# Layer 0 of a four-layer graph network: sums of exponentials by thirds of a half, and the last 20 keys held three times in row groups

## The chip, the cores and the metric

The kernel runs on one core of a Trainium2 chip. The time is that of one execution on the device in microseconds (us); the median of three runs is given. One execution more was taken with the hardware profiler, and every line of a profile shown here is of such an execution. The engines are PE (TensorE, with its weight loads, PEld), DVE (VectorE), ACT (ScalarE), POOL (GpSimd) and SP (SyncE, which here issues most DMAs).

## What is computed

Four layers work on 2708 nodes with 512 features each, with one adjacency matrix `adj` (2708 x 2708, about 1.2% ones and a full diagonal). After each layer, x is added and the rows are normalized. The change is in layer 0 alone, an encoder and a decoder over the same attention. Cut to what matters, with N = 2708, H = 4 heads, D = 128:

```python
Xw  = einsum('hnd,hde->hne', Xh, W)
f1  = einsum('hnd,hd->hn', Xw, V[:, 0, :, 0])
f2  = einsum('hnd,hd->hn', Xw, V[:, 1, :, 0])
sig = sigmoid(f1[:, :, None] + f2[:, None, :])
att = softmax(where(adj != 0, adj * sig, -inf))      # over the keys; both patterns are adj
Xa  = einsum('hij,hjd->hid', att, Xw)                # attention pass a
emb = mlp_block(batchnorm(Xa))                       # elu, a product with 512 x 512, batch norm
Y   = einsum('hij,hjd->hid', att, emb)               # attention pass c, the same att
out = mlp_block(elu(Y @ W.T))
x   = layernorm(x + out)
```

Layers 1 (mean over neighbours), 2 and 3 (attention over all nodes) follow; nothing in them is touched.

## The kernel before, in words

**Tiles.** Keys (the index j that is summed over) lie on the partitions, in 22 tiles: 21 of 128 keys and a last one of 20, since 2708 = 21 x 128 + 20. Queries (i) lie along the free axis, in two halves of 1354. The four heads are taken in two pairs. So `attention_pass` (from line 270) has four rounds, (half 0, pair 0), (half 0, pair 1), (half 1, pair 0), (half 1, pair 1), and each goes over the 22 key tiles `jt`. It runs twice: as pass a with the values `xw`, and as pass c with `emb`.

**One key tile.** `form` loads a 128 x 1354 piece of the adjacency (L300, on SP's queue; four buffers in pass a). With pair 0 in pass a it first turns zeros into a very negative number on DVE (L303, L304) and stores the piece to DRAM for later rounds (L307, on POOL's queue). Then ACT makes tanh of f1 + f2 for both heads (L313, two instructions), DVE combines it with the adjacency (L321), and ACT takes the exponential (L322). The result `t`, 128 keys x 2 heads x 1354 queries, has four buffers. PE then makes the weighted sums (L366): for each head three products of 452 or 450 columns, with a 128 x 128 piece of the values as weights, accumulated over the 22 tiles in PSUM. The accumulators are three tiles po0, po1, po2, one for each third of the half, each with one bank for each head of the pair.

**Sums of exponentials.** In pass a alone, PE also adds up the exponentials over the keys (L389): for each head four products of 340 columns, with a 128 x 32 block of ones as weights. Each quarter of the half goes to its own 32 PSUM rows (0, 32, 64, 96), and so to its own 32 columns of the array. With pair 0 this is done for every tile. With pair 1 it is done for each of the first six tiles, and then once for two tiles, which DVE adds up first in place (L383). The last tile is the second of such a two.

**The end of a round.** In pass a, `keep` copies the accumulators to `ft` (L466: the first and last thirds on DVE, the middle ones on ACT), takes the sums at least at a tiny number (L473), sends them through DRAM to be inverted and spread over the partitions (L476 to L483, then `spread_sums`, L260 and L264), and leaves eight small steps (L490 and L491: scale a quarter of a head, take its statistics) for the next round's tiles. In (half 0, pair 1) it also makes a small product, ps_beta (L434), in the slot of po0. In the last round there is no next one: maxima (L505), reciprocals (L506), a product that spreads a row over the partitions (L512, in two of the accumulator slots in turn) and the eight steps (L520, L521) are done on the spot. In pass c, `decode` scales the accumulators on DVE (L660), adds the shift and masks (L672), and goes on to ps_y (L676), the elu (L403 to L408), and after pair 1 the decoder's product (L687).

**Kept tiles.** In pass a the exponentials of some key tiles are stored to DRAM (L358): tiles 5, 13 and 21 of pair 0, and 3, 9, 15 and 21 of pair 1. Pass c reloads these (L360) and makes the others anew. The last tile, 21, is so kept in all four rounds.

**What sets the order.** The program is written once in the order of the work; a tile framework's scheduler puts each engine's instructions in a fixed order when the kernel is built, from dependencies, priorities and the buffers of each pool. [...] A PSUM accumulator is taken again when all that read it are done.

The dimensions behind the lines that are changed:

```python
NHALF, HB, HP = 2, 3, 2            # halves, thirds of a half, heads of a pair
HW = 2 * ((N + 3) // 4)            # 1354
BW = 2 * ((HW + 2 * HB - 1) // (2 * HB))   # 452
SQ = 4
SW = 2 * ((HW + 2 * SQ - 1) // (2 * SQ))   # 340
```

Layers 2 and 3 already hold the values of the last 20 keys in four copies, at partitions 0, 32, 64 and 96, and make their products there in four row groups (L1090, records marked `20*128`).

Of the kernel before, what the change touches and what calls it, by code (L numbers as in the profile page):

```python
# [8 lines left out]
F32 = mybir.dt.float32  # L9
# [4 lines left out]
ALU = mybir.AluOpType  # L14
# [3 lines left out]
P = 128  # L18
# [3 lines left out]
TINY = 1e-30  # L22
# [7 lines left out]
def gnn_stack_kernel(  # L30
# [25 lines left out]
    nc = tc.nc  # L56
    N, F = x.shape
    H = w0.shape[1]
    C = F // P
    NT = (N + P - 1) // P  # L60
    NFULL = N // P
    BLOCKS = [(i * P, min(P, N - i * P)) for i in range(NT)]
    BANK = 512

    const = ctx.enter_context(tc.tile_pool(name="const", bufs=1))
    big = ctx.enter_context(tc.tile_pool(name="big", bufs=1))
# [59 lines left out]
    CHUNKS = [(h0 + q0, w) for (h0, _), ch in zip(HSPAN, HCH) for q0, w in ch]  # L126
    NCH = len(CHUNKS)

    SQ = 4
    SW = 2 * ((HW + 2 * SQ - 1) // (2 * SQ))  # L130
    SCH = [[(q * SW, min(SW, w - q * SW)) for q in range(SQ)] for _, w in HSPAN]

# [18 lines left out]
    with ExitStack() as l0:  # L151
# [7 lines left out]
        }  # L159
        f1_d = dram.tile([H, N], F32, name="f1_d")  # L160

        SR = SQ * SW // 17
        assert SR <= P and SR * 17 == SQ * SW
        sum_d = dram.tile([H, NHALF, SQ, SW], F32, name="sum_d")
        rs_d = dram.tile([H, NHALF, SQ, SW], F32, name="rs_d")

# [3 lines left out]
        ones32 = p0.tile([P, 32], F32, name="ones32")  # L170
        nc.vector.memset(ones32, 1.0)
        f2h = p0.tile([P, NT, H], F32, name="f2h")

        bm1 = p0.tile([P, C], F32, name="bm1")
        nc.vector.tensor_scalar(bm1, prm_sb[:, MB_DEC, :], 1.0, None, ALU.subtract)
# [10 lines left out]
        def project(att, psum):  # L186

            held = p0.tile([P, C, F], F32, tag="mlp_w", name="held").rearrange("p c f -> p (c f)")  # L190
            w0x = held[:, : H * (P + 2)].rearrange("p (h e) -> p h e", h=H)
            nc.sync.dma_start(w0x[:, :, :P], w0)
            v12 = att.tile([P, H, 2], F32, tag="v12", name="v12", bufs=1)
            nc.sync.dma_start(v12[:, :, 0], v1)
            nc.sync.dma_start(v12[:, :, 1], v2.rearrange("(h e) -> e h", h=H))
            for c in range(C):
                nc.sync.dma_start(xT_sb[:, c, :], xT[c * P : (c + 1) * P, :])
            pv = psum.tile([P, H, 2], F32, tag="psm0", name="pv")
            for h in range(H):
                nc.tensor.matmul(  # L200
                    pv[:, h, :], w0T_sb[:, h, :], v12[:, h, :], start=True, stop=True
                )
            nc.vector.tensor_copy(w0x[:, :, P:], pv)
            wv1 = held[:, H * (P + 2) : H * (2 * P + 2)].rearrange("p (h e) -> p h e", h=H)
            nc.vector.tensor_copy(wv1, w0x[:, :, P : P + 1].to_broadcast([P, H, P]))
            f1b = att.tile([P, HP, HW], F32, tag="f1b", name="f1b")
            for k in range(HP):
                for q, (q0, w) in enumerate(HCH[0]):
                    pf = psum.tile([P, HP, BANK], F32, tag=f"po{q}", name="pf")[:, k, :]
                    nc.tensor.matmul(  # L210
                        pf[:, :w], wv1[:, k, :], xT_sb[:, k, q0 : q0 + w], start=True, stop=True
                    )
                    copy = nc.scalar.copy if q % 2 else nc.vector.tensor_copy
                    copy(f1b[:, k, q0 : q0 + w], pf[:, :w])
            for ci, (c0, w) in enumerate(CHUNKS):
                pf = psum.tile([P, BANK], F32, tag=f"psm{ci % 2}", name="pf")
                for h in range(H):
                    nc.tensor.matmul(
                        pf[32 * h : 32 * h + 32, :w],
                        wv1[:, h, :32],  # L220
                        xT_sb[:, h, c0 : c0 + w],
                        start=True,
                        stop=True,
                    )
                f1c = att.tile([P, BW], F32, tag="rs", name="f1c")
                nc.vector.tensor_copy(f1c[:, :w], pf[:, :w])
                nc.gpsimd.dma_start(f1_d[:, c0 : c0 + w], f1c[0 : 32 * H : 32, :w])
            for jt, (j0, n) in enumerate(BLOCKS):
                pxw = psum.tile([P, H // HP, BANK], F32, tag=f"po{jt % HB}", name="pxw")
                pv = pxw[:, :, : HP * (P + 2)].rearrange("p a (k e) -> p a k e", k=HP)  # L230
                for h in range(H):
                    nc.tensor.matmul(
                        pv[:n, h // HP, h % HP, :],
                        xT_sb[:, h, j0 : j0 + n],
                        w0x[:, h, :],
                        start=True,
                        stop=True,
                    )
                copy = nc.vector.tensor_copy if jt % 3 == 2 else nc.scalar.copy
                copy(  # L240
                    xw[:n, jt, :].rearrange("p (a k d) -> p a k d", a=H // HP, k=HP),
                    pv[:n, :, :, :P],
                )
                nc.vector.tensor_scalar(
                    f2h[:n, jt, :].rearrange("p (a k) -> p a k", k=HP),
                    pv[:n, :, :, P + 1],
                    0.5,
                    None,
                    ALU.mult,
                )  # L250
            return f1b

        def spread_sums(att, hf, p):
# [16 lines left out]
        def attention_pass(values, first, att, psum, finish, f1b=None):  # L270
# [23 lines left out]
            def form(hf, p, jt, att, prepare, f1b, tv):  # L294
# [3 lines left out]
                a = att.tile([P, HW], F32, tag="a", name="a", bufs=4 if first else 3)  # L298
                src = adjT if prepare else adj_d
                nc.sync.dma_start(a[:n, :w], src[j0 : j0 + n, h0 : h0 + w])  # L300
                if prepare:
                    z = att.tile([P, HW], F32, tag="z", name="z", bufs=1)
                    nc.vector.tensor_scalar(z[:n, :w], a[:n, :w], 0.0, None, ALU.is_equal)  # L303
                    nc.vector.scalar_tensor_tensor(  # L304
                        a[:n, :w], z[:n, :w], -BIG, a[:n, :w], ALU.mult, ALU.add
                    )
                    nc.gpsimd.dma_start(adj_d[j0 : j0 + n, h0 : h0 + w], a[:n, :w])  # L307
                if not first and p == (jt in KEPT[0]):
                    count(hf, jt, att, a)

# [14 lines left out]
            for hf, (h0, w) in enumerate(HSPAN):  # L325
                for p in range(H // HP):
# [20 lines left out]
                    for jt, (j0, n) in enumerate(BLOCKS):  # L347
# [5 lines left out]
                        tv = t[:n, :, :w]  # L353
                        kept = kept_d.get((hf, p, jt))
                        if kept is None or first:
                            form(hf, p, jt, att, prepare, f1b, tv)
                            if kept is not None:
                                nc.gpsimd.dma_start(kept[:n, :, :w], tv)  # L358
                        else:
                            nc.sync.dma_start(tv, kept[:n, :, :w])  # L360
                            if p == 0 and jt in KEPT[1]:
                                count(hf, jt, att)
                        for k in range(HP):
                            h = HP * p + k
                            for q, (q0, qw) in enumerate(HCH[hf]):
                                nc.tensor.matmul(  # L366
                                    po[HB * k + q][:, :qw],
                                    values[:n, jt, h * P : (h + 1) * P],
                                    t[:n, k, q0 : q0 + qw],
                                    start=(jt == 0),  # L370
                                    stop=(jt == NT - 1),
                                )
# [73 lines left out]
        with (  # L446
# [7 lines left out]
            def keep(hf, p, po, sums):  # L454
# [15 lines left out]
                if not final:  # L470
                    for k in range(HP):
                        h = HP * p + k
                        nc.vector.tensor_scalar(  # L473
                            sm[k][:, :SW], sums[k][:, :SW], TINY, None, ALU.max
                        )
                        nc.gpsimd.dma_start(sum_d[h, hf], sm[k][0 : 32 * SQ : 32, :SW])  # L476
                    part = slice(HP * p, HP * (p + 1)), hf
                    few = att.tile([SR, HP, 17], F32, tag="few", name="few", bufs=1)
                    wide = "h r w -> h (r w)"
                    cut = "h (s e) -> s h e"  # L480
                    nc.sync.dma_start(few, sum_d[part].rearrange(wide).rearrange(cut, s=SR))
# [20 lines left out]
                    )  # L502
                for k in range(HP):
                    h = HP * p + k
                    nc.vector.tensor_scalar(sm[k][:, :SW], sums[k][:, :SW], TINY, None, ALU.max)  # L505
                    nc.vector.reciprocal(sm[k][:, :SW], sm[k][:, :SW])  # L506
                    nc.gpsimd.dma_start(rs_d[h, hf], sm[k][0 : 32 * SQ : 32, :SW])
                    for r, (q0, qw) in enumerate(SCH[hf]):
                        pb = psum.tile(
                            [P, HP, BANK], F32, tag=f"po{1 + (SQ * k + r) // 2 % 2}", name="pb"  # L510
                        )[:, r % 2, :]
                        nc.tensor.matmul(  # L512
                            pb[:, :SW],
                            sel[:, r * P : (r + 1) * P],
                            sm[k][:, :SW],
                            start=True,
                            stop=True,
                        )
# [37 lines left out]
        with (  # L556
# [36 lines left out]
            for ci, (c0, w) in enumerate(CHUNKS):  # L593
# [34 lines left out]
                while turned < NT and sum(BLOCKS[turned]) <= c0 + w:  # L628
# [3 lines left out]
                        nc.tensor.transpose(tp[:n, c, :], ft[:, c, j0 : j0 + n], ident)  # L632
                    nc.scalar.copy(emb[:n, turned, :], tp[:n].rearrange("p c d -> p (c d)"))
                    turned += 1


            scale2, mean2 = batch_scale(stats, MG_ENC, "bn2")
# [231 lines left out]
    GW = max(w for _, w in GSPAN)  # L869
    GB = max(len(g) for g in GROUPS)  # L870

    Q = 32
    REST = N - NFULL * P
    assert 0 < REST <= Q and C * Q == P
    quarters = const.tile([P, C, Q], F32, name="quarters")
    for c in range(C):
        nc.vector.tensor_tensor(
# [535 lines left out]
```

## Time and profile before

| what (before) | value |
|---|---|
| median of three runs | 3387.1 us (3385.58 to 3390.83) |
| the profiled execution's own time | 3383.28 us |
| its span, from the first to the last instruction | 3381.5 us |
| mean granted clock of PE, as a share of full | 0.984 |
| PE busy (matmul records) | 3304.0 us |
| DVE, ACT, POOL busy | 1988.8, 1339.6, 127.6 us |
| pass a, from its first weighted sum to its last sum of exponentials | 53.7 to 586.6 us |
| pass c, from its first weighted sum to its last | 703.6 to about 1181 us |
| layer 1's first product | 1244.0 us |

A group's row gives line, engine, operation, what is written and read (`20*128` is 20 active rows and 128 active columns of the array), sizes and count, then the busy time and the mean of one in ns, then the engine's idle time just before and what ended most of it. An fp32 product is two records. Matmuls are pipelined, and their ends are modelled; for the pace of PE, starts are to be compared, not lengths.

### The profile page before, as it was taken

What the parts mean: (1) busy time and instruction counts of PE and PEld (TensorE: products, weight loads), DVE (VectorE), ACT (ScalarE), POOL (GpSimd) and SP (SyncE); (2) the same over time, 40 slices, a digit from 0 to 9 for tenths busy, and PEclk for the clock granted to TensorE, in tenths of its full rate; (3) what the DMA queues carried; (4) which work ended last, traced back from release to release, by engine and by line L of the source; (5) the groups of instructions that cost most, each with busy time, mean ns of one, the idle gap of its engine ahead of it and who ended that gap; (6) DMA issues with size and microseconds to landing.
All of it is one profiled execution on the core that took longest, in us unless ns stands there. A gap on an engine that the chain in (4) does not pass through costs nothing.

```text
span 3381.5 us, 30504 instructions
## 1 busy us (share of the span) xinstructions
PE 3304.0 (98%) x10981; PEld 1761.1 (52%) x10981; DVE 1988.8 (59%) x3227; ACT 1339.6 (40%) x1491; POOL 127.6 (4%) x205
## 2 busy tenths in 40 slices
PE   8999999999999989999999999999999999999998
PEld 4444444544444445886555555444455555555554
DVE  7867977767687585445136666777253442543533
ACT  6877887568858743001133333333011010110110
POOL 1100100000000000000010000000000000000001
PEclk9998999999999999999999999999999999999999
DMA  7655753335524331550034444554111111111100
GB/s 279 246 164 166 276 184 114 120 103 168 184 82 160 126 106 61 140 136 19 0 114 125 116 127 128 145 148 112 58 50 35 44 33 44 37 33 44 35 23 19
DMA packets 167483, 364.03 MB, mean 108 GB/s; under 512 B 20374, under 2 KB 111194, under 8 KB 164100
## 3 DMA queue, kind: packets, MB, share of 16 engines
q1 hardware_dynamic: 152596, 298.43, 29.3%
q0 software_dynamic: 14736, 63.66, 5.0%
q8 instruction: 86, 1.41, 0.2%
q14 instruction: 65, 0.53, 0.0%
HBM read 298.34 MB, written 63.35 MB: 107 GB/s over the span
## 4 chain that ended last, share of the span: by engine, by line
PE 74%; issue 15%; DVE 6%; DMA 2%; ACT 2%; POOL 1%; SPq 0%; POOLq 0%; DVEq 0%; ACTq 0%
PE po L1090 22%; PE ps_s L996 17%; PE po L366 8%; PE ps_nb L842 7%; PE ps_wide L908 4%; PE ps_hid L113 2%; PE ps_sup L1233 2%; DVE t L321 2%; PE ps_o L1168 2%; PE ps_dec L687 2%; PE ps_mlp L601 1%; DMA a<-adj_d 1%; POOL adj_d L307 1%; PE ps_s L991 1%; ACT t L313 1%
## 5 line engine op out<-in xcount | busy, mean ns | idle before, releaser
L321 DVE SCALAR_TENSOR_TENSOR t<-t,a 128x2708 f32<-128x2708 f32 (+1 forms) x162 | 479.3, 2975 | 144.8 <-ACT t L313 143.3
L313 ACT ACTIVATE t<-f1b,f2h 128x1354 f32<-128x1354 f32 (+1 forms) x324 | 445.3, 1414 | 91.2 <-PE psm L389 47.1
L366 PE MATMUL po<-t,xw 128*128 128x452 f32 (+3 forms) x1056 | 433.0, 561 | 3.9 <-ACT t L322 3.9
L366 PE MATMUL po<-t,emb 128*128 128x452 f32 (+3 forms) x1056 | 416.3, 552 | 10.7 <-ACT t L322 9.2
L322 ACT ACTIVATE t<-t 128x2708 f32<-128x2708 f32 (+1 forms) x162 | 396.7, 2452 | 52.0 <-DVE t L321 50.5
L1090 PE MATMUL po<-sup,e 128*128 128x512 f32 x882 | 410.0, 601 | 5.2 <-DVE e L1277 5.2
L1090 PE MATMUL po<-e,xs 128*128 128x384 f32 (+1 forms) x1176 | 407.5, 489 | 0.0
L996 PE MATMUL ps_s<-q,hT 128*128 128x384 f32 (+1 forms) x1176 | 403.5, 489 | 0.0
L1331 DVE SCALAR_TENSOR_TENSOR e<-a_cols,ps_s 128x384 f32<-128x384 f32 (+1 forms) x154 | 85.6, 556 | 419.7 <-PE ps_s L996 396.6
L366 PEld LDWEIGHTS po<-t,emb 128*128 128x128 f32 (+1 forms) x1056 | 201.6, 193 | 220.1 <-issue 199.2
L366 PEld LDWEIGHTS po<-t,xw 128*128 128x128 f32 (+1 forms) x1056 | 197.8, 193 | 224.9 <-issue 211.4
L996 PEld LDWEIGHTS ps_s<-q,hT 128*128 128x128 f32 x1176 | 222.6, 190 | 161.5 <-issue 6.2
L1090 PEld LDWEIGHTS po<-e,xs 128*128 128x128 f32 x1176 | 221.6, 190 | 157.2 <-issue 6.0
L1090 PEld LDWEIGHTS po<-sup,e 128*128 128x128 f32 x882 | 162.0, 192 | 176.8 <-issue 148.3
L996 PE MATMUL ps_s<-hT 128*128 128x384 f32 (+1 forms) x672 | 229.2, 488 | 1.0 <-ACT sup L1240 0.7
L93 ACT ACTIVATE ln_rstd<-ln_rstd 128x1 f32<-128x1 f32 x88 | 17.2, 201 | 497.4 <-DVE ln_rstd L92 496.9
L1273 ACT ACTIVATE a_cols<-a_cols,neg_big 128x384 f32<-128x384 f32 (+1 forms) x154 | 94.8, 616 | 249.7 <-DMA a_cols<-in_adjT_dram 208.4
L842 PE MATMUL ps_nb<-hid_hi,at 128*128 128x512 f32 x484 | 188.1, 390 | 0.4 <-DVE at L836 0.4
L842 PE MATMUL ps_nb<-hid_lo,at 128*128 128x512 f32 x484 | 187.8, 389 | 0.0
L1067 ACT COPY nmax<-pb 128x384 f32<-128x384 f32 (+1 forms) x14 | 6.7, 479 | 430.5 <-PE pb L1054 349.8
L996 PEld LDWEIGHTS ps_s<-hT 128*128 128x128 f32 x672 | 125.8, 190 | 97.1 <-issue 18.0
L1085 DVE TENSOR_TENSOR acc<-acc,e 128x384 f32<-128x384 f32 (+2 forms) x294 | 162.9, 554 | 12.3 <-ACT e L1075 2.3
(223 smaller groups left out, 3474.1 us busy)
## 6 DMA issues: line engine op xcount, KB each, us to landing
a<-adj_d SPq DMA_DIRECT2D x116, 677.0 KB
a_cols<-in_adjT_dram SPq DMA_DIRECT2D x378, 192.0 KB
a<-in_adjT_dram SPq DMA_DIRECT2D x42, 677.0 KB
adj_d<-a POOLq DMA_DIRECT2D x42, 677.0 KB, 4.5
raw<-in_adjT_dram SPq DMA_DIRECT2D x105, 256.0 KB
kept<-t POOLq DMA_DIRECT2D x10, 1354.0 KB, 6.6
t<-kept SPq DMA_DIRECT2D x10, 1354.0 KB
a_cols<-in_adjT_dram SPq DMA_DIRECT2D x63, 202.0 KB
```

The costliest lines, as they stand in the source:

```text
L113: nc.tensor.matmul(ps[:n], xt[:, c, :n], w[:, c, :], start=(c == 0), stop=(c == C - 1))
L313: nc.scalar.activation(tv[:, k, :], f1b[:n, k, :w], AF.Tanh, bias=f2h[:n, jt, h : h + 1], scale=0.5,)
L321: nc.vector.scalar_tensor_tensor(tv, tv, GUARD, ab, ALU.add, ALU.mult)
L322: nc.scalar.activation(tv, tv, AF.Exp, scale=0.5)
L366: nc.tensor.matmul(po[HB * k + q][:, :qw], values[:n, jt, h * P : (h + 1) * P], t[:n, k, q0 : q0 + qw], start=(jt == 0), stop=(jt == NT - 1),)
L842: nc.tensor.matmul(pos[it], at, half[:, jt, :], start=(jt == 0 and k == 0), stop=(jt == NT - 1 and k == 1),)
L908: nc.tensor.matmul(ps[:, :width], w(c, o), xt(c), start=(c == 0), stop=(c == C - 1),)
L996: nc.tensor.matmul(ps[:, :w], keys[:, c, j0 : j0 + P], st["q"][:, c, :], start=(c == 0), stop=(c == C - 1),)
L1085: nc.vector.tensor_tensor(acc, acc, e[:m], ALU.add)
L1090: nc.tensor.matmul(out, lhsT, rhs, start=(k == 0), stop=(k == NT - 1))
L1273: nc.scalar.activation(a, a, AF.Identity, bias=neg_big[: a.shape[0]], scale=1.0e30)
L1331: nc.vector.scalar_tensor_tensor(e, a, 2.0, ps, ALU.mult, ALU.add)
```

## The change

Two things are changed in layer 0.

The sums of exponentials are made by thirds of a half (`SQ = HB = 3`, so `SW = 452`) where they were made by quarters. For each head there are three products of 452 columns on PSUM rows 0, 32 and 64. All that follows from it has thirds too: maxima and reciprocals on 96 rows of 452, the small steps that are left for the next round (six of 452 or 450 columns for eight of 340 or 334), the statistics, and the way through DRAM (113 rows of 12 numbers for each head in place of 80 rows of 17). In the last round the spreading product has a slot of its own for each of its six results.

The last 20 keys lie in three copies, at partitions 0, 32 and 64 (84 rows with the gaps, `HR`). `form` loads the adjacency's last 20 rows three times and 12 rows of other keys into each of the two gaps, five DMAs for one; tanh, combination and exponential run on 84 rows. The values get their copies by DMAs on POOL's queue (`copies`: `xw` and `f2h` after the projection, `emb` after the encoder). Pass c reloads the last tile three times. In the weighted sums of the last tile, third q of the queries is made on row group q, so that the three products of a head use three row groups of the array; the columns and the accumulators are the same as before. The sums of exponentials still take the first 20 rows alone.

```diff
+    Q = 32
+    REST = N - NFULL * P
...
-    SQ = 4
+    SQ = HB
...
-        SR = SQ * SW // 17
-        assert SR <= P and SR * 17 == SQ * SW
+        SR = next(k for k in range(P, 0, -1) if SQ * SW % k == 0)
+        SE = SQ * SW // SR
+        SP = 32 * SQ
...
+        nc.vector.memset(f2h[:, NT - 1, :], 0.0)
+        HR = (HB - 1) * Q + REST
+        def copies(rows):
+            for r in range(1, HB):
+                nc.gpsimd.dma_start(rows[r * Q : r * Q + REST], rows[:REST])
...
+            copies(xw[:, NT - 1, :])
+            copies(f2h[:, NT - 1, :])
...
                 nc.sync.dma_start(a[:n, :w], src[j0 : j0 + n, h0 : h0 + w])
+                if n < P:
+                    for r in range(HB):
+                        if r > 0:
+                            nc.sync.dma_start(
+                                a[r * Q : r * Q + n, :w], src[j0 : j0 + n, h0 : h0 + w]
+                            )
+                        if r + 1 < HB:
+                            nc.sync.dma_start(
+                                a[r * Q + n : (r + 1) * Q, :w], src[: Q - n, h0 : h0 + w]
+                            )
+                    n = HR
...
-                            form(hf, p, jt, att, prepare, f1b, tv)
+                            rows = n if n == P else HR
+                            form(hf, p, jt, att, prepare, f1b, t[:rows, :, :w])
...
-                            nc.sync.dma_start(tv, kept[:n, :, :w])
+                            for r in range(0, P if n == P else HB * Q, P if n == P else Q):
+                                nc.sync.dma_start(t[r : r + n, :, :w], kept[:n, :, :w])
...
                             for q, (q0, qw) in enumerate(HCH[hf]):
+                                r = 0 if n == P else q * Q
                                 nc.tensor.matmul(
                                     po[HB * k + q][:, :qw],
-                                    values[:n, jt, h * P : (h + 1) * P],
-                                    t[:n, k, q0 : q0 + qw],
+                                    values[r : r + n, jt, h * P : (h + 1) * P],
+                                    t[r : r + n, k, q0 : q0 + qw],
...
-                    nc.vector.reciprocal(sm[k][:, :SW], sm[k][:, :SW])
-                    nc.gpsimd.dma_start(rs_d[h, hf], sm[k][0 : 32 * SQ : 32, :SW])
+                    nc.vector.reciprocal(sm[k][:SP, :SW], sm[k][:SP, :SW])
+                    nc.gpsimd.dma_start(rs_d[h, hf], sm[k][0:SP:32, :SW])
                     for r, (q0, qw) in enumerate(SCH[hf]):
-                        pb = psum.tile(
-                            [P, HP, BANK], F32, tag=f"po{1 + (SQ * k + r) // 2 % 2}", name="pb"
-                        )[:, r % 2, :]
+                        slot = SQ * k + r
+                        pb = psum.tile([P, HP, BANK], F32, tag=f"po{slot // 2}", name="pb")
+                        pb = pb[:, slot % 2, :]
...
+            copies(emb[:, NT - 1, :])
```

## The prediction

> **What bounds the kernel now.** I read the page first: which engine is full, and where the clock falls.
>
> ```profile
> PE 3304.0 (98%) x10981; PEld 1761.1 (52%) x10981; DVE 1988.8 (59%) x3227; ACT 1339.6 (40%) x1491; POOL 127.6 (4%) x205
> ...
> PEclk9998999999999999999999999999999999999999
> ...
> L366 PE MATMUL po<-t,xw 128*128 128x452 f32 (+3 forms) x1056 | 433.0, 561 | 3.9 <-ACT t L322 3.9
> L366 PE MATMUL po<-t,emb 128*128 128x452 f32 (+3 forms) x1056 | 416.3, 552 | 10.7 <-ACT t L322 9.2 <-DVE ot L660 1.4
> ```
>
> TensorE (PE) is full, and the weighted sums of both attention passes (L366) waited only 3.9 and 10.7 us in all. Layer 0 takes the first 1,240 us; the change touches only its passes, a (53.7 to 586.6 us) and c (703.6 to 1181 us). In pass a a PE microsecond counts in full, unless a wait takes its place. Next, the timeline of PE where one pair of heads ends and the next begins (start, length, engine, line, what, records):
>
> ```profile
> 171.32 4.82 PE L366 MATMUL po<-t,xw 128*128 128x452 f32 x12
> 176.07 1.35 PE L389 MATMUL psm<-t,ones 128*32 128x340 f32 x16
> 177.35 5.89 PE L366 MATMUL po<-t,xw 20*128 20x452 f32 x12
> 183.17 2.49 PE L389 MATMUL psm<-t,ones 20*32 20x340 f32 x16
> 185.59 7.58 PE L366 MATMUL po<-t,xw 128*128 128x452 f32 x12
> ```
>
> From start to start, a full tile of keys costs 4.75 us of weighted sums (12 records, two for each fp32 product, 0.377 us apart) and 1.28 us of sums of exponentials. The last 20 keys cost as many records on 20 of 128 rows, and from there all slows. The table by stretch (PE busy, ..., granted clock, DMA) tells why:
>
> ```profile
> 171.32:177.35 6.03, 6.03 (x32) 2.62 (x29) 4.94 (x2) 5.20 (x4) 0.00 (x0) 1.00 0.36 116
> 177.35:181.00 3.65, 3.65 (x14) 1.90 (x11) 0.32 (x1) 3.65 (x3) 0.00 (x0) 0.99 0.60 193
> 181.00:185.59 4.59, 4.59 (x21) 1.04 (x19) 2.52 (x5) 2.18 (x4) 0.19 (x1) 0.50 0.01 1
> 185.59:191.00 5.41, 5.41 (x11) 2.52 (x8) 5.27 (x3) 4.58 (x3) 0.97 (x2) 0.50 0.20 23
> ```
>
> After 3.65 us of 20-row products, with PE busy throughout, the clock is halved, and stays so into the next tile. The same follows the other 20-row tiles (half clock in 310.6 to 327.7 and in 812.4 to 815.8, for two). I call these places ends, and the start of the last 20 keys T.
>
> [...] layer 3's last keys (8 records of 384 columns) start at 2564.27 and the next product at 2565.13, 0.86 us against 2.58 for full rows. Three column groups no run shows yet. [...]
>
> **Sums in thirds: a loss on the path.** Before, eight 340-column products fill four column groups: four rounds for 16 records, 1.28 us. After, six 452-column products fill three: again four rounds, now wider. The nearest row is f1 (L218), 16 records of 450 or 452 columns in four groups:
>
> ```profile
> 32.61 1.72 PE L218 MATMUL pf<-xT_sb,held 128*32 128x452 f32 x16
> 34.26 2.84 PE L232 MATMUL pxw<-held,xT_sb 128*128 128x130 f32 x23
> ```
>
> Start to start 1.65 us, so 0.37 more a group. Below, 0.30, if only part of the width shows; [...] I take 0.37. The 1152 records of L389 are 72 groups: 26.6 us. The built order also splits two of the first four groups (1 product, 12 projections, 5 products): 0.85 each for an extra round, 1.7. In the second pair of heads of each half PE waited for exponentials 3.9 us in all; ACT's pair of tiles (2 x (2 x 1.41 + 2.45) = 10.5 us) then has more room: 2.9 us absorbed. Sum: **+25.4**.
>
> **The last 20 keys in row groups: PE time.** Twelve records in three groups are four rounds of 0.377 plus 0.22 of start (0.86 - 2 x 0.32 in the layer-3 row): 1.73 us in place of 4.75, at all eight ends. But what comes next was hidden under those 3 us.
>
> **End of pass a's first pairs (T = 177.35, 451.02).** PE after: T+1.73, sums to T+3.4, first product of the new pair to T+4.15; the second needs accumulator po1, copied out by ACT (L466). ACT's order, unchanged by the build: tanh of a tile whose buffer comes free at T, then both copies.
>
> ```profile
> 177.24 2.46 ACT L322 ACTIVATE t<-t 128x2708 f32<-128x2708 f32 x1 [0.69 <-DVE t L321]
> 179.61 2.72 ACT L313 ACTIVATE t<-f1b,f2h 128x1354 f32<-128x1354 f32 x2
> 182.24 0.95 ACT L466 COPY ft<-po 128x452 f32<-128x452 f32 x2
> ```
>
> That is T+4.9 to T+5.85, and it doesn't move, for what feeds it is released at T. So PE stands 1.75 us, and its five other products end at T+9.7. In T to T+5.9 PE then has 1.73 us on 60 rows, 1.65 on 20, 0.75 in full and a stall: [...] I expect the clock to halve again, for a shorter time (5 us at half = 2.2 to 2.5 lost[...]). With 2.2, T+11.9; before, 193.09 = T+15.74. Gain 3.8, and the last group's 0.37 is hidden by the wait: **-4.2 each**.
>
> **End of the first half (T = 306.60).** The sums need the last two tiles added (L383), which can't start before T, as it overwrites what PE reads until then:
>
> ```profile
> 306.78 2.97 DVE L383 TENSOR_TENSOR t<-t 20x2708 f32<-20x2708 f32 x1
> 309.67 1.55 DVE L304 SCALAR_TENSOR_TENSOR a<-z,a 128x1354 f32<-128x1354 f32 x1
> 311.15 0.61 DVE L466 COPY ft<-po 128x452 f32<-128x452 f32 x1
> ```
>
> Before, PE reached its sums at T+5.4, with all that past. After, it is ready at T+1.73 and starts them at about T+3.75 (the build puts a 0.86 step ahead of the add); then one product, then ps_beta (L434, 32 records, 3.6 us at full clock, as at 612.5) which needs the copies, T+7.1; with the five other products T+14.6, sums T+15.9 at 1.28. [...] the clock halves here as well (estimate 3.5 lost): T+19.2 against 330.45 = T+23.85: **-4.7**.
>
> **End of pass a (T = 579.21).** The chain from the add through L466, the maxima, two reciprocals (2.2 us at 340 columns, 3.0 at 452) to the last statistics is DVE's. It starts when the add does, at T+0.2; 1.5 more of reciprocals, 0.7 less for six scalings and statistics (452 columns, 1.24 a pair) in place of eight (1.01). The accumulator slots no longer repeat, which saves the 0.8 that DVE waited for PE. **0**.
>
> **Pass c.** First end: DVE copies out (L660) at T+2.07 when its tile work is done, po0 is free at T+3.4; gain of 2 us less stalls and the same half clock: **-0.7**. Second and third: PE already waits for these copies.
>
> ```profile
> 1069.63 2.98 DVE L321 SCALAR_TENSOR_TENSOR t<-t,a 128x2708 f32<-128x2708 f32 x1 [4.35 <-ACT t L313]
> 1072.75 3.83 DVE L660 SCALAR_TENSOR_TENSOR ot<-po,bn_scale,rb 128x452 f32<-128x452 f32 x6
> ```
>
> DVE is held by L321 from T+0.2 to T+3.2, then copies; PE, which in its own timeline starts at 1074.94 after 0.71 us of waiting for L660, starts at T+5.5 whenever it ended: **0**. The last: DVE has been idle, so the first copy moves from 1180.22 (T+3.3) to T+1.9, with a little less half clock after it: **-2**.
>
> **Costed at nothing.** The DMAs of copies sit on SP behind loads that wait for buffers some tiles ahead, and the reloads of kept tiles (three for one) likewise. On POOL four copies stand before the fourth tile's store: 4 x 0.55 us later, under the room of a tile of 6.4 us; bare, 2.2. ACT and DVE on 84 rows in place of 20 take the same (L321: 2.91 to 2.98 for both). The few scalings of pass a ride in DVE's idle time.
>
> **Sum.** 25.4 - 2 x 4.2 - 4.7 - 0.7 - 2 = **+9.6**. Of the profiled execution (3383.3 us: span 3381.5, 1.8 around it) that makes 3392.9; it lay 3.8 under the median shown, 3387.1, so I name **3396.7**.
>
> **Rivals.** (1) The clock holds: [...] all ends keep full clock: 2 x 2.2 + 3.5 saved in pass a, some 1.7 at each of three ends of pass c: -13, **3384**, not slower. [...] (2) The full 3 us are won at each end because the copies run earlier than I place them: about 1.75 x 2 + 2 + 2 x 2 more, **3387**. (3) Ends gain nothing, as new waits and longer half clock eat all; the sums stay: **3406**, or up to 3414 if row groups ran one after another, which layer 3 speaks against. [...]
>
> **Chances.** Forecast (+7 to +14) 0.48; (1) 0.17; (2) 0.15; (3) 0.15; (4) 0.05. Within 0.2% (6.8 us, about what can be told from no change) falls most of (1) and (2): same 0.28; of (1) a tail falls below: faster 0.08; slower 0.64. The range reaches into (1) and (3): 3384 to 3406. Faster and same together hold less than the slower cases, whose own range is 3394 to 3406.
>
> **What would show it.** L389's groups at 1.65 us start to start, right[...]. The 20-row tiles at 1.7 us, right; 4.7, no concurrency. At T+4 a wait of PE for ACT's L466, at the half's end for the add, in pass c for L660; without them rival 2. Clock of 0.5 within 7 us after T; if 1.0, rival 1. Wrong altogether if pass a doesn't grow.

## The result, and the profile after

The changed kernel took 3401.8 us (median of 5, 3396.4 to 3404.0) against 3387.1 for the kernel before: ratio 1.0043 (95% interval 1.0028 to 1.0058), 14.7 us slower. The profiled execution took 3396.4 us (span 3394.6), 13.2 us more in span than before's. After's lines are numbered anew: L398 is the old L366 (weighted sums), L421 L389 (sums), L415 L383 (add), L498 L466 (copies in pass a), L350 and L351 L321 and L322, L695 L660, L707 L672, L711 L676, L438 L406 (elu), L466 L434 (ps_beta). Each experiment's kernel is numbered anew again.

Of the page, TensorE (PE) and the two groups of weighted sums:

```profile
PE 3294.7 (97%) x10689; PEld 1743.8 (51%) x10689; DVE 1988.5 (59%) x3211; ACT 1342.2 (40%) x1491; POOL 129.9 (4%) x211
...
L398 PE MATMUL po<-t,emb 128*128 128x452 f32 (+3 forms) x1056 | 403.2, 552 | 20.0 <-ACT t L351 15.2
...
L398 PE MATMUL po<-t,xw 128*128 128x452 f32 (+3 forms) x1056 | 412.1, 553 | 3.2 <-ACT ft L498 2.3
```

PE is still full. Pass a waits as little as before (3.2 us for 3.9), now for L498. Pass c waits 20.0 us where it waited 10.7. PE's timeline at the first end:

```profile
184.16 1.79 PE L398 MATMUL po<-t,xw 20*128 20x452 f32 x12
185.88 1.71 PE L421 MATMUL psm<-t,ones 20*32 20x452 f32 x12
187.52 1.02 PE L398 MATMUL po<-t,xw 128*128 128x452 f32 x2
189.67 5.57 PE L398 MATMUL po<-t,xw 128*128 128x452 f32 x10 [1.13 <-ACT ft L498]
195.17 1.72 PE L421 MATMUL psm<-t,ones 128*32 128x452 f32 x12
```

From start to start: the last 20 keys 1.72 us, the sums 1.64, then two records, the wait for ACT's copy, and the rest. In the table by stretch the second part has a clock of 0.82; the same place in (half 1, pair 0) has 1.00:

```profile
187.52:196.82 9.30, 8.17 (x27) 3.15 (x24) 7.84 (x7) 7.14 (x6) 1.01 (x2) 0.82 0.34 88
...
458.08:469.22 11.14, 10.02 (x51) 3.59 (x48) 9.20 (x9) 10.49 (x8) 1.00 (x2) 1.00 0.34 92
```

The clock records of both traces hold 1.00 and 0.50 alone, so the missing share gives the half clock: 2 x (1 - 0.82) x 9.30 = 3.3 us here, none there. The end of the first half, from its sums:

```profile
313.96 1.72 PE L421 MATMUL psm<-t,ones 128*32 128x452 f32 x12 [1.41 <-DVE t L415]
315.61 1.02 PE L398 MATMUL po<-t,xw 128*128 128x452 f32 x2
317.04 5.19 PE L466 MATMUL ps_beta<-prm_sb,enc_w 128*128 128x1 f32 x32 [0.41 <-DVE ft L498]
322.10 5.90 PE L398 MATMUL po<-t,xw 128*128 128x450 f32 x10
```

And the third end of pass c:

```profile
1084.10 1.87 PE L711 MATMUL ps_y<-ot,w0T_sb 128*128 128x452 f32 x2 [1.96 <-DVE ot L707]
...
1095.00 1.02 PE L711 MATMUL ps_y<-ot,w0T_sb 128*128 128x450 f32 x2 [0.64 <-DVE elu_r L438]
1100.38 5.13 PE L398 MATMUL po<-t,emb 128*128 128x452 f32 x8 [4.35 <-ACT t L351]
```

At this end VectorE (DVE) does the following:

```profile
1082.17 1.28 DVE L695 SCALAR_TENSOR_TENSOR ot<-po,bn_scale,rb 128x452 f32<-128x452 f32 x2 [5.96 <-PE po L398]
...
1083.97 2.46 DVE L695 SCALAR_TENSOR_TENSOR ot<-po,bn_scale,rb 128x452 f32<-128x452 f32 x4
...
1094.87 2.97 DVE L350 SCALAR_TENSOR_TENSOR t<-t,a 128x2708 f32<-128x2708 f32 x1
```

The 20.0 us from T (1080.35) to 1100.38 hold all records of ps_y and 12 of the new round's weighted sums; before, they held those of ps_y and 22. ps_y now stands ahead of the new round's products and waits for VectorE. VectorE copies the accumulators from T+1.8 on and makes the next tile only at T+14.5, so the new round's exponentials come 4.35 us late. At the first and the second end PE waits as well, for the elu and for the copies:

```profile
830.40 2.77 PE L711 MATMUL ps_y<-ot,w0T_sb 128*128 128x452 f32 x4 [3.44 <-DVE elu_r L438]
...
931.32 6.01 PE L398 MATMUL po<-t,emb 128*128 128x452 f32 x8 [3.34 <-DVE ot L695]
```

Where the 13.2 us are, from starts in both timelines of PE (an end of pass a runs from T to the third tile of the next round, or to the encoder's first product; an end of pass c from T to the eighth tile of the next round) and the half clock in each stretch:

| stretch | before, us (half clock) | after | difference |
|---|---|---|---|
| to the first weighted sum | 53.7 | 53.6 | -0.1 |
| pass a between ends | 449.5 (0) | 467.6 (0) | +18.1 |
| pass a, its four ends | 95.5 (41.0) | 80.7 (10.2) | -14.7 |
| encoder | 104.9 (0) | 108.7 (10.2) | +3.8 |
| pass c, its first three ends | 169.2 (10.2) | 179.1 (20.5) | +9.9 |
| pass c, the rest | 358.2 (13.7) | 356.7 (6.8) | -1.5 |
| after the decoder's last product | 2150.5 (43.2) | 2148.3 (37.7) | -2.2 |

At the first three ends of pass c the half clock doubled; half of the added 10.2 us, 5.1, is about half of their 9.9.

### The profile page after: what moved, and what is told of

It reads as the page before. It is cut to its first block, busy times and chain, and to the rows that moved or that the text cites. A ratio compares the mean times of both kernels' runs of the same rounds, so it can differ in the third digit from the quotient of the medians.

```text
span 3394.6 us, 29963 instructions
## 1 busy us (share of the span) xinstructions
PE 3294.7 (97%) x10689; PEld 1743.8 (51%) x10689; DVE 1988.5 (59%) x3211; ACT 1342.2 (40%) x1491; POOL 129.9 (4%) x211
## 4 chain that ended last, share of the span: by engine, by line
PE 76%; issue 12%; DVE 6%; DMA 2%; ACT 2%; POOL 1%; SPq 0%; POOLq 0%; DVEq 0%; ACTq 0%
PE po L1120 22%; PE ps_s L1026 18%; PE po L398 9%; PE ps_nb L877 6%; PE ps_wide L938 4%; DVE t L350 2%; PE ps_hid L118 2%; PE ps_sup L1263 2%; PE ps_o L1198 2%; PE ps_mlp L635 2%; PE ps_dec L722 1%; DMA a<-adj_d 1%; PE psm L421 1%; ACT t L351 1%; ACT t L342 1%
## 5 line engine op out<-in xcount | busy, mean ns | idle before, releaser
L350 DVE SCALAR_TENSOR_TENSOR t<-t,a 128x2708 f32<-128x2708 f32 (+1 forms) x162 | 479.0, 2974 | 153.0 <-ACT t L342 151.2
L351 ACT ACTIVATE t<-t 128x2708 f32<-128x2708 f32 (+1 forms) x162 | 397.2, 2454 | 72.1 <-DVE t L350 71.3
L398 PE MATMUL po<-t,emb 128*128 128x452 f32 (+3 forms) x1056 | 403.2, 552 | 20.0 <-ACT t L351 15.2
L398 PE MATMUL po<-t,xw 128*128 128x452 f32 (+3 forms) x1056 | 412.1, 553 | 3.2 <-ACT ft L498 2.3
L398 PEld LDWEIGHTS po<-t,emb 128*128 128x128 f32 (+1 forms) x1056 | 195.6, 193 | 224.0 <-issue 195.8
L398 PEld LDWEIGHTS po<-t,xw 128*128 128x128 f32 (+1 forms) x1056 | 189.6, 191 | 225.5 <-issue 208.7
L98 ACT ACTIVATE ln_rstd<-ln_rstd 128x1 f32<-128x1 f32 x88 | 17.2, 201 | 497.5 <-DVE ln_rstd L97 497.0
L1026 PEld LDWEIGHTS ps_s<-hT 128*128 128x128 f32 x672 | 125.9, 190 | 97.1 <-issue 18.2
```

Of the source, the lines that this page charges most:

```text
L350: nc.vector.scalar_tensor_tensor(tv, tv, GUARD, ab, ALU.add, ALU.mult)
L351: nc.scalar.activation(tv, tv, AF.Exp, scale=0.5)
L398: nc.tensor.matmul(po[HB * k + q][:, :qw], values[r : r + n, jt, h * P : (h + 1) * P], t[r : r + n, k, q0 : q0 + qw], start=(jt == 0), sto ...
L1026: nc.tensor.matmul(ps[:, :w], keys[:, c, j0 : j0 + P], st["q"][:, c, :], start=(c == 0), stop=(c == C - 1),)
```

## The experiments

My theory after this comparison: the sums in thirds cost PE's time and are the loss; the row groups win in pass a and lose in pass c. Rivals: that the row groups cost it, that pass c only met half clock in other places, and, on the side of the gain, that it is PE's shorter products. All ratios are to the kernel before on the same chip, with 95% intervals; 0.001 is 3.4 us.

**The parts alone.** First the thirds without row groups (the last tile as before):

```diff
-                if n < P:
+                if False:
...
-                                r = 0 if n == P else q * Q
+                                r = 0
```

> The sums of exponentials in thirds alone: the last 20 keys are made as in the kernel before, one copy, 20 rows for all three thirds. Theory A (the two halves of the change add up, by the stretches of the trace of after): 72 groups of sums x 0.366 us = 26.4, less 2 to 4 us of waits for exponentials in the second pairs that the longer tiles swallow: +22 to +25 us against before, all of it in pass a, and pass c as before within 2 us. Rival B (the thirds cost little by themselves, and what was lost comes from the row groups): +12 us or less.

Measured 3409.9 us, ratio 1.0083 (1.0070 to 1.0096): +28 us, somewhat above theory A. Then the row groups without the thirds (`SQ = 4`, the slots of pb as before):

> The last 20 keys in three row groups alone, in both passes; the sums stay in quarters. Theory A: the three ends of rounds in pass a gain 5 to 6 us each, the last about 1, pass c loses 8 as in after (its order of instructions is the one of after), and half clock may cost up to 4 in the encoder: -9 us against before, -5 to -13. Rival B (the ends gain only what thirds hide, or the halved clock eats them): between -4 and +4.

Measured 3380.0, 0.9992 (0.9984 to 1.0000): -3 us, within the range of rival B. The whole change in pass a, with pass c as before:

```diff
...
-                                r = 0 if n == P else q * Q
+                                r = q * Q if first and n < P else 0
...
-            copies(emb[:, NT - 1, :])
```

> The whole change in pass a, but pass c takes the last 20 keys as the kernel before does (one copy, 20 rows), and emb gets no copies. Its built order in pass c is that of before, instruction for instruction on TensorE. Theory A (the 8 us that pass c lost in after come from the row groups there, by the changed order and the waits for VectorE and ScalarE): pass c as before within 2 us, and the whole +4 to +8 against before, some 8 us under after. Rival C [...]: within 3 us of after, +12 to +17.

Measured 3390.4, 1.0025 (1.0015 to 1.0036): +8.5, just above A and below C. And this with `SQ = 4`:

> Row groups for the last 20 keys in pass a alone, sums in quarters, pass c as before. Theory A: the gains of the ends without the thirds and without the loss in pass c: -17 us against before, -12 to -20. Rival D (without the thirds the sums end sooner, and the new rounds wait so much longer for the copies of the accumulators that most of it goes): -8 us or less of a gain.

Measured 3374.0, 0.9974 (0.9966 to 0.9981): -9.

So the thirds are the loss (rival B of the first falls), and the row groups are no loss in pass a. In pass c they cost 1.0018 in both pairs (1.0043 to 1.0025, and 0.9992 to 0.9974): 6 us, in favour of theory A. The second pair is clear of noise (0.0018 with some 0.0011 either way, an estimate from the two intervals), the first by itself hardly (0.0018 either way). The traces agree: pass c took 535.8 and 534.2 us with row groups in it, and 527.4 to 531.4 in the four with 20 rows and the order of before. But the gain with quarters was half of what I expected, nearer the rivals B and D. With thirds the row groups of pass a win 0.0058 (20 us), with quarters 0.0026 (9): the parts don't add up. In the traces the gap is 9.0 us (14.6 and 5.6 in span), and it doesn't lie where the row groups work: at the four ends of pass a they win nearly the same, 11.8 us with thirds (95.0 to 83.2) and 10.5 with quarters (95.5 to 85.0). It lies in the encoder, by 8.5 us. The encoder took 113.2 us with 19.5 us of half clock in the run of the thirds alone and 104.9 with none in before, but 108.8 and 108.9 with 10.2 in the two runs with row groups. Less half of their half clock all four are 103.5 to 104.9 us. So in these traces the gap is a matter of half clock in a stretch that the row groups don't touch; whether it falls so in the other executions, which were not traced, is open.

**Work or clock?** At the four ends of pass a half clock fell by 30.8 us, from 41.0 to 10.2. At half clock (0.50 from 185.59 to 191.00 in before) records of 452 columns start 0.75 us apart for 0.38 at full, so half the time is lost, and this is worth 15.4 us. The ends won 14.7 although they hold ten of the longer groups (3.7 us). That leaves 3.0 us for the 12 us of products that row groups take off PE there (an estimate from the table). So I left PE's work alone and gave the last tile all rows:

```diff
+        nc.vector.memset(xw[:, NT - 1, :], 0.0)
...
+                if n < P:
+                    nc.sync.dma_start(a[n:, :w], src[: P - n, h0 : h0 + w])
+                    n = P
...
-                                    values[:n, jt, h * P : (h + 1) * P],
-                                    t[:n, k, q0 : q0 + qw],
+                                    values[:, jt, h * P : (h + 1) * P],
+                                    t[:, k, q0 : q0 + qw],
```

> The kernel before, but its last 20 keys are computed as a full tile of 128 rows: 108 more keys of other tiles stand below them with values of zero (and zeros in the block of ones), so they add nothing. TensorE's instructions and their order are those of before; the 12 products take 4.75 us as before; only the number of active rows differs, and what ACT, VectorE and the DMAs carry for that tile. Theory E (what the row groups won at the ends of rounds is mostly the clock, that the 20-row products had halved, and hardly TensorE's own 3 us, for which the next round has no accumulators yet): the half clock of 10.2, 17.1, 10.2 and 3.4 us at the ends of pass a goes but for what ps_beta causes, 15 to 18 us less, and 2 to 5 more in pass c: -14 to -22 us against before, more than the row groups in pass a win with the same quarters (9.5). Rival F (the win is TensorE's shorter products; the clock falls back anyway at the change of rounds): between -4 and +2.

Measured 3356.7, 0.9924 (0.9911 to 0.9937): -26 us, more than expected, and the lowest ratio of all. All 10,981 records of PE stand in the same order as before's. PE's timeline at the first end:

```profile
176.06 4.82 PE L375 MATMUL po<-t,xw 128*128 128x452 f32 x12
180.80 1.35 PE L398 MATMUL psm<-t,ones 128*32 128x340 f32 x16
182.09 4.82 PE L375 MATMUL po<-t,xw 128*128 128x452 f32 x12
```

The tile takes the pace of any other, 6.03 us, and the next one starts without a wait: ACT's and VectorE's copies are hidden under it. T to the third tile is 18.1 us for 23.1, though PE does nothing less. Of the four ends only ps_beta's keeps 3.4 us of half clock (its stretch, 300.30 to 324.10, has a clock of 0.93; those of the first and third end 1.00); they take 78.4 us (before 95.5). The first three ends of pass c have none and take 163.9 us (before 169.2). Rival F falls. The same with thirds:

> The sums of exponentials in thirds as in the change, the last 20 keys as a full tile with zeros for values, as in the run beside it (108 more keys with values of zero; nothing is added to the result). With the clock kept up in both, the difference of the two is the thirds by themselves: 72 x 0.366 = 26.4 us less 2 to 4 of waits in the second pairs = +22 to +25 us over the kernel with quarters and full rows, if their price is TensorE's time (theory A). If the 26 to 28 us that the thirds cost on their own had a part of clock in it (the encoder's stretch was 8 us longer there, with half clock in 19 us of it), under +20.

Measured 3385.0, 1.0001 (0.9992 to 1.0009), so 1.0001 / 0.9924 = 1.0078 for the thirds with a full last tile: 26 us, a little above theory A. In the two traces it is 24.2 us from the first weighted sum to the encoder (552.21 and 528.05). The clock isn't quite equal there: 9.8 us of half clock with thirds for 3.4 with quarters, worth 3.2 us. So most of the price is TensorE's time.

How many rows keep the clock up? The full tile cut to 64 and to 32 rows in products and sums (against the kernel with full rows):

```diff
-                                    values[:, jt, h * P : (h + 1) * P],
-                                    t[:, k, q0 : q0 + qw],
+                                    values[: n if n == P else 64, jt, h * P : (h + 1) * P],
+                                    t[: n if n == P else 64, k, q0 : q0 + qw],
...
-                                    ones20 if whole is t and n < P else ones32,
+                                    (ones20 if whole is t and n < P else ones32)[:m],
```

> As the kernel with a full last tile, but its products and sums take 64 of the 128 rows (20 keys and 44 others with values of zero). Same instructions, same order, same pace of TensorE; only the number of active rows differs. Theory E1 [...]: no half clock at the ends of pass a but for ps_beta, within 4 us of full rows, about -26 us against before. Rival E2 [...]: back to -8 to 0.

> The same with 32 of the 128 rows (20 keys and 12 others with values of zero), a quarter of the array. Theory E1 [...]: the clock halves at all ends as it did with 20 rows, -5 to +3 us against before. Rival E3 (it was the 20 rows' uneven fill, or only the number of products[...]): -20 us or less.

64 rows: 3363.3, 0.9928 (0.9906 to 0.9950), as full rows. 32 rows: 3382.9, 0.9990 (0.9982 to 0.9998), 3 us under before, within E1's range. PE's timelines at the first end, of 64 and of 32 rows:

```profile
175.76 4.81 PE L375 MATMUL po<-t,xw 64*128 64x452 f32 x12
180.51 1.35 PE L398 MATMUL psm<-t,ones 64*32 64x340 f32 x16
181.79 4.82 PE L375 MATMUL po<-t,xw 128*128 128x452 f32 x12
```

```profile
177.13 6.41 PE L375 MATMUL po<-t,xw 32*128 32x452 f32 x12
183.47 2.49 PE L398 MATMUL psm<-t,ones 32*32 32x340 f32 x16
185.89 7.05 PE L375 MATMUL po<-t,xw 128*128 128x452 f32 x12
```

PE is busy throughout in both. With 64 rows the tile takes 4.75 us from start to start and the next one 4.74; with 32 rows they take 6.34 and 6.98. The granted clock over these whole executions is 0.991 with 64 rows and 0.982 with 32 (0.990 with 128). In the three kernels every engine has the same instructions in the same order, and ACT, VectorE and the DMAs carry the same 128 rows. So neither their work nor PE's order makes the difference; the number of PE's active rows does. Rivals E2 (-8 to 0 us with 64 rows, measured -24) and E3 (-20 or less with 32, measured -3) fall. What happens between 32 and 64 rows was not tried.

Then both, row groups with all 32 rows of each at work in pass a, full rows in pass c (again against the kernel with full rows):

```diff
+                                part = slice(32 * q, 32 * q + 32) if first and n < P else slice(P)
...
-                                    values[:, jt, h * P : (h + 1) * P],
-                                    t[:, k, q0 : q0 + qw],
+                                    values[part, jt, h * P : (h + 1) * P],
+                                    t[part, k, q0 : q0 + qw],
```

> Row groups and full activity together: in pass a the last 20 keys in three row groups of all 32 rows (the 12 gap rows with values of zero, so 96 rows at work), their sums on 128 rows with zeros in the block of ones; in pass c a full last tile. Quarters. Nothing is added to the result by the zeros. Theory E (the clock was most of the win, TensorE's own time the rest): the ends of pass a lose their half clock and keep the shorter products, 1 us at two ends and up to 2 at the other two under full rows: -3 to -6 us against full rows, -30 to -34 against before. Rival K [...]: +3 to +8 against full rows.

Measured 3366.4, 0.9942 (0.9927 to 0.9957): about 6 us behind full rows by the ratios. The intervals overlap and the two ran on different chips, so that it is slower isn't certain; but the 3 to 6 us under full rows that theory E forecast are out of reach, and rival K's range fits. From its table by stretch, T of the first and the third end to the product after the wait:

```profile
175.33:181.22 5.89, 4.06 (x35) 1.41 (x31) 3.94 (x7) 5.89 (x6) 1.14 (x2) 1.00 0.39 120
...
440.31:446.44 6.13, 3.07 (x32) 1.11 (x28) 5.43 (x3) 5.99 (x6) 0.00 (x0) 1.00 0.49 169
```

PE is busy for 4.06 of 5.89 us and 3.07 of 6.13, and waits for ACT's copy in the rest (1.77 and 3.07 us). The first end is 0.9 us shorter than with full rows (17.2 for 18.1). At the second (26.9 for 23.8, with a wait of 3.32 us for VectorE's add) the clock from 298.70 to 307.56 is 0.81, and the sums after the wait take 2.43 us for 1.28. At the third (19.9 for 18.2) the 14 records after the wait take 7.20 us; 14 x 0.377 would be 5.28. Of the 3 us that row groups take off PE at an end little is won, as the next round waits for its accumulators (1.77 and 3.07 us).

**Order in pass c.** The build had changed PE's order at the first three ends of pass c. The whole change, with precedence for the next round's first tiles there:

```diff
-                            form(hf, p, jt, att, prepare, f1b, t[:rows, :, :w])
+                            with ExitStack() as soon:
+                                if not first and jt < 4:
+                                    soon.enter_context(tc.high_priority())
+                                form(hf, p, jt, att, prepare, f1b, t[:rows, :, :w])
```

> The changed kernel, but in pass c the first four tiles of a round are given precedence when the instructions are put in order, so that VectorE and ACT make them before they take up the decoder's small steps of the round that ended. Theory G (the 6 to 8 us that the row groups cost in pass c come from the order: at three ends VectorE copies the accumulators and makes the elu first, and the next round's exponentials come late, 4.35 us of waiting at one place): -5 to -9 us against after, +6 to +9 against before. Rival H (the accumulators cannot be copied out sooner in any order, and what precedence gives the tiles it takes from the copies): within 3 us of after, or slower.

Measured 3400.0, 1.0049 (1.0038 to 1.0060): nothing gained, as rival H had it. Yet the trace had shortened the third end (43.6 us for 49.3) and lengthened the first (48.7 for 45.3, with 13.7 us of half clock). That is one bad order, not all, so I tried two that keep closer to before's (`jt < 2`, and `jt < 4` with `offset=60`):

> The changed kernel with precedence for the first two tiles of a round in pass c (four in the run before). At the second end TensorE's order is now that of before, at all three VectorE makes one tile more ahead of the accumulators' copies. Theory L (in pass c the loss is not the order: the row groups take 3 us of work off TensorE, the copies of the accumulators come no sooner, and what was work is now a wait[...]): within 4 us of after whatever the order, +11 to +19 against before. Theory G (the order): one that is close to before's gets back most of the 6 us: +6 to +10.

> The changed kernel with a weaker precedence for the first four tiles of a round in pass c: at the first and third end TensorE's order is that of before but for one or two products, and VectorE makes the next tile between the accumulators' copies and the decoder's small steps; the second end is as in after. Theory L: within 4 us of after, +11 to +19 against before. Theory G: +6 to +10.

Measured 3393.1, 1.0022 (1.0014 to 1.0030), and 3386.2, 1.0009 (1.0000 to 1.0018): 7 and 11 us less than after, the latter under the kernel without row groups in pass c (1.0025) by 5 and better than theory G's own range. Pass c by itself took 528.6 and 526.3 us in their traces (after 535.8, before 527.4). Theory L falls, and my reading of the run before with it: the order was the loss. The third end of the last one, PE and VectorE:

```profile
1070.12 6.55 PE L401 MATMUL po<-t,emb 128*128 128x452 f32 x24 [0.68 <-ACT t L351]
1079.99 8.00 PE L401 MATMUL po<-t,emb 128*128 128x452 f32 x16 [3.33 <-DVE ot L698]
```

```profile
1075.08 2.98 DVE L350 SCALAR_TENSOR_TENSOR t<-t,a 128x2708 f32<-128x2708 f32 x1 [4.35 <-ACT t L342]
1077.97 3.06 DVE L698 SCALAR_TENSOR_TENSOR ot<-po,bn_scale,rb 128x452 f32<-128x452 f32 x5
1080.95 2.97 DVE L350 SCALAR_TENSOR_TENSOR t<-t,a 128x2708 f32<-128x2708 f32 x1
```

PE waits 3.33 us for the copies, which stand behind one tile, but then has products for 8 us, as VectorE makes the next tile before it goes on. The three ends take 168.4 us (after 179.1, before 169.2).

## Why the prediction was right, and where it was not

Its sum, +9.6, was right in sign and nearly in size (+13.2 on the profiled executions, +14.7 by the medians), but pass a came out 9 us better than forecast, and pass c 11 us worse. That these two errors nearly cancel is luck.

- **Sums in thirds, +25.4: right.** A group takes 1.65 us, as f1's row had it. With a full last tile the thirds cost 26 us. Two small terms inside were off. To split the early groups cost 0.2 us (predicted 1.7): from their first record to the first weighted sum it is 13.82 us for 12.86, 0.73 of it for two longer groups. And waits absorbed 3.9 (60 groups between the ends x 0.366 = 22.0, measured 18.1) where 2.9 was forecast. The gain of three column groups, which no run before had shown, is now in the trace: 12 records at 0.377 would take 4.52 us one after another, and a group takes 1.65, 2.74 times less.
- **The 20-key tile at 1.73: right**, 1.72 at the first end.
- **First ends of pass a, -4.2 each: right in kind.** PE waits for ACT's L498, 1.13 us at the first where 1.75 was forecast. The new round's first sums start at T+11.0 and T+9.5 (forecast T+11.9). The clock halved at one and for 3.4 us (0.82 from 187.52 to 196.82), not at both for 5 (1.00 from 458.08 to 469.22).
- **End of the first half, -4.7: right.** The sums wait for the add, then ps_beta for the copies; PE's second tile starts at T+18.8 (forecast T+19.2; its own terms, T+15.9 and an estimate of 3.5, make 19.4). **End of pass a, 0: right**, -0.6.
- Together the four ends were to gain 13.1, less 3.7 for the ten longer groups in them: -9.4. They gained 14.7, as half clock fell by 31 us. In the five traces that have both changes in pass a the four ends took 80.7 to 83.2 us, so this isn't the chance of one execution. The half clock at the ends is the first mis-sized term, with the early groups: pass a grew by 3.3 us where 12.3 was forecast (2.4 of this for the early groups, which lie ahead of its first weighted sum).
- **Pass c, -2.7: the step that failed.** It said of the second and third end: "DVE is held by L321 from T+0.2 to T+3.2, then copies; PE [...] starts at T+5.5 whenever it ended". At the third end that holds only for the order of before. The build, with shorter products at the end of a round, put VectorE's copies there ahead of the next tile, at T+1.8, and ps_y ahead of the new round's products, and left the new round without exponentials for 4.35 us. At the second, PE did start at T+5.1, but after a wait of 3.34 us (0.71 before), and with 6.8 us of half clock for 3.4; the first, forecast at -0.7, had a wait for the elu of 3.44 us that no term held. The three ends came out at +2.1, +2.1 and +5.6 us, and pass c grew by 8.3. In the order closest to before's (the last experiment) the three ends changed by -1.5, +1.1 and -0.3 us against before, and PE started at T+5.1 at the third. So the step's reasoning holds where the order does; its premise, that the order stays, was wrong. The last end, -1.9, was as forecast.
- **Not in the sum:** the encoder, +3.8, and the rest of the program, -2.2, which the change doesn't touch. In seven traces whose encoder has the same instructions on PE in the same order as before's, it took 104.9 to 108.9 us with 0 to 10.2 us of half clock. After's order there differs in places; its 108.7 lies among them, and less half of its half clock it is 103.5 us, no more than before's 104.9. So these +3.8 are half clock.
- Of the rivals, (1) was half right: at some ends the clock held (1.00 at the third of pass a). (3), "ends gain nothing", came as near the result by number (3406, where the forecast was 3396.7 and 3401.8 was measured), but not by its reason: the ends gained in pass a and lost in pass c. Nor does its 3406 follow from the prediction's terms: with no gain at any end they make 3387.1 + 25.4 = 3412.5.

What the prediction saw but didn't draw on: it named the halved clock after the 20-row tile, and took it as something that shorter products would shorten. In pass a it was the larger part of what the row groups won (15.4 us of the 18.4 net of the longer groups), and 108 rows with values of zero won more, 26 us in the whole kernel.

## What to carry to other kernels

When PE is busy and its clock is halved, try more rows in the thin tile: here, to pad it from 20 to 128 with zero values made it no longer (4.74 us from start to start, for 5.82 with 20 rows and half clock in them) and was worth more than packing it (ratio 0.9924 against 0.9974). To make the last tile of a round shorter won PE's time here only as far as the accumulators came free sooner; the rest of the work turned into a wait (1.13 us at the first end of pass a, 3.34 at the second of pass c). And a changed duration reorders what a scheduler places far from the edit: compare the built order at every place where a shortened step ends, before costing it at nothing.

## What was unexpected of the hardware

PE's busy time didn't tell the clock; the number of active rows went with it. With 64 of 128 rows the twelve records of the last tile took 4.75 us, as with 128 (4.74), and with 32 they took 6.34, with PE busy throughout in both. Rows aren't all of it: in the run with full rows, the stretch that holds the 32 records of ps_beta, of 128 rows but one column each, has a clock of 0.93 (300.30 to 324.10). In before, 32 such records at 612.51 left it at 1.00 (612.51 to 619.50), so not each such group goes with half clock.

The same stretch has more or less half clock in different executions, as the encoder did (0 to 10.2 us in the seven traces with before's order on PE); before alone ran from 3376.1 to 3389.1 us in 32 executions on one chip. That half clock is all of this scatter wasn't tried.

How long half clock lasted differed too: 3.4 us at the first end of after (189.3 to 192.8), and 13.7 at the first end of pass c in the first order experiment (823.2 to 836.8).
